# Attention with a depthwise convolution: key blocks in batches of twelve instead of nine

## The chip, the cores and the metric

The kernel runs on one core of a Trainium2 chip. The metric is the device time of one execution in microseconds (us). TensorE (PE) multiplies matrices; its weight loads (PEld) are shown apart. VectorE (DVE), ScalarE (ACT) and GpSimd (POOL) do the rest of the arithmetic, SyncE (SP) only issues DMAs. ScalarE and GpSimd issue DMAs too. Each engine works through its own instructions in order; one that waits holds up everything behind it on that engine.

## The reference

For 4 images `x` of 384 channels and 48 x 48 = 2304 tokens, with 8 heads of 48 channels:

```python
local = conv_general_dilated(x, conv_w, padding='SAME', feature_group_count=C)   # 7 x 7, depthwise
local = local * inv + shift                                                      # batch norm
x_norm = layernorm(x_flat)
q, k, v = split(x_norm @ qkv_w.T + qkv_b)
q = q + layernorm(local_flat)
attn = softmax(q @ k.T * scale)
out = x_flat + (attn @ v) @ proj_w.T + proj_b
```

Everything is float32.

## The kernel before, in words

**Stages.** An image is taken in two stages. The key stage goes through six groups of 384 tokens: keys, values and raw queries are projected (L715), and for images 2 to 4 the output projection of the image before is done beside it. Then the attention goes through five groups of query tokens, of 384 (the first), 480, 480, 480 and 480 columns. The groups are numbered t = 0 to 19 over the four images; t = 0 to 4 are image 1, t = 5 to 19 images 2 to 4.

**Batches.** In one query group each of the four pairs of heads (p = 0 to 3) meets 18 blocks of 128 keys, 72 blocks in all. They are done in 8 batches of 9 blocks, a batch belonging to one pair. A batch has two phases. In `score_batch`, TensorE makes the scores of a block (`score`, L1142): three passes (high x high, high x low, low x high parts in float32r), each for two heads at a time, one head on the upper 64 rows of the array and one on the lower. The two heads' scores take two of the eight PSUM banks, in turn, so four blocks fit. The exponentials go from there to `weights_of` in SBUF: for the first five blocks (`SPLIT`) at once, one ScalarE instruction for both heads (L1158); of the sixth the first half at once; the rest waits in `exps` until weighing. `weights_of` has 11 half-block slots, used in turn. In `weigh_batch`, TensorE multiplies the weights of each block with the values (`weigh`, L1179): full float32, the two heads on the left and right 64 columns of the array. After each `weigh` one waiting exponential is issued, into slots that have become free. The batch's sums are copied out by ScalarE (`sums_out`, L1027 and L1037), and the second part of a pair is added to the first by DVE in the next batch (`sums_add`, L1046).

**Easing.** In some batches (`eased`; all of them for t from 4 on) the third block's second half is copied by DVE from PSUM to SBUF (L1162), and ScalarE makes its exponential in place later (L1154). Scoring then finds the banks free earlier.

**Points.** The order of all engines but GpSimd is written out by hand. Each batch has four points, q = 0 to 3: in mid-scoring, at the end of scoring, in mid-weighing, at the end. `steps_of(t)` hangs other work on points (s, q): the norm of the next image's x (in the last groups of images 1 to 3), the norm of the next group's convolution (`Norm`: sums, a turn through DRAM and back, centring, squares, root, Newton step), query stacks, the division by the softmax sums. At each point `convolve` also issues some of the 7 x 7 convolution for the next group on DVE (L347, 144 instructions a group). How many is worked out ahead by `plan`: every point has a `room` in us (`spare`, and `spare_at_keys` for the key stage's points), a norm needs its group's convolution finished at a due point, and the plan spreads the instructions in proportion to room at the smallest rate that meets the next ten due points.

**Query stacks.** For each pair, `high_queries` (ScalarE, L998) and `low_queries` (DVE, L1003, and DMAs on SP, L1008 and L1010) make a tile `qs` of high, low and shifted parts. The tag `qs` has four buffers, shared with the residuals (`load_residual`) and fetched outputs (`fetch`) of the key stage.

**Keys.** A pair's keys are three stacks of 6 blocks. Three stack tiles are in SBUF; in the key stage pair 0's stacks are made there, those of pairs 1 to 3 are stored to DRAM (`keys_out`, GpSimd's DMAs at L749 to L778). Afterwards `next_keys` loads one stack after another (L787) into the tile whose blocks have been scored. Loads 3 and 4 of each image are issued by ScalarE, all others by GpSimd. `keep_stack` (L782) stores pair 0's stacks for the later groups.

## Time and profile before

| | |
|---|---|
| runs | 2703.12, 2704.47, 2705.36 us; median 2704.47 |
| profiled execution | 2702.29 us, span in the profile 2700.0 us |
| granted TensorE clock | 1.00 |
| TensorE, DVE, ScalarE, GpSimd busy | 2688.3, 2353.5, 1648.4, 599.4 us |
| image 1, attention | from 146.9 to 683.4 us |
| attention of images 2, 3, 4 | from 825.0, 1484.1 and 2141.5 us |

In the tables of groups a row gives line, engine and operation, output and inputs with their shapes, the count, then busy time in us and the mean of one in ns, then the idle time of the engine just before these instructions and what ended it. In a timeline a row is the start in us, the time from the first start to the last end, and what ran how often; square brackets hold the idle time before it and the releaser. Matmuls overlap, so a single one lasts longer than the distance between two.

### The profile page before, as it was taken

What the parts mean: (1) busy time and instruction counts of PE and PEld (TensorE: products, weight loads), DVE (VectorE), ACT (ScalarE), POOL (GpSimd) and SP (SyncE); (2) the same over time, 40 slices, a digit from 0 to 9 for tenths busy, and PEclk for the clock granted to TensorE, in tenths of its full rate; (3) what the DMA queues carried; (4) which work ended last, traced back from release to release, by engine and by line L of the source; (5) the groups of instructions that cost most, each with busy time, mean ns of one, the idle gap of its engine ahead of it and who ended that gap; (6) DMA issues with size and microseconds to landing.
All of it is one profiled execution on the core that took longest, in us unless ns stands there. A gap on an engine that the chain in (4) does not pass through costs nothing.

```text
span 2700.0 us, 45552 instructions
## 1 busy us (share of the span) xinstructions
PE 2688.3 (100%) x16442; PEld 1543.1 (57%) x16442; DVE 2353.5 (87%) x4105; ACT 1648.4 (61%) x2487; POOL 599.4 (22%) x1073
## 2 busy tenths in 40 slices
PE   9999999999999999999999999999999999999999
PEld 6565555555566655555555655555555665555555
DVE  8999999999999999888999999888899899887212
ACT  4466776777325777777622767777753376766662
POOL 4541111102462111011165111101126401110110
PEclk9999999999999999999999999999999999999999
DMA  8454444645465545355456553545636644445442
GB/s 177 93 159 134 132 114 132 154 116 153 125 155 159 141 116 146 117 153 139 123 146 156 155 150 111 150 123 140 150 102 166 166 131 131 139 124 147 136 129 94
DMA packets 160395, 370.43 MB, mean 137 GB/s; under 512 B 58544, under 2 KB 107504, under 8 KB 160160
## 3 DMA queue, kind: packets, MB, share of 16 engines
q0 software_dynamic: 71072, 277.78, 36.3%
q1 hardware_dynamic: 83456, 79.29, 13.1%
q10 hardware_dynamic: 5632, 10.36, 1.2%
q8 instruction: 132, 2.16, 0.3%
q14 instruction: 103, 0.84, 0.1%
HBM read 258.14 MB, written 64.14 MB: 119 GB/s over the span
## 4 chain that ended last, share of the span: by engine, by line
PE 90%; DVE 6%; DMA 2%; issue 1%; ACT 0%; SPq 0%; POOL 0%; DVEq 0%; ACTq 0%; POOLq 0%
PE banks L1179 41%; PE banks L1142 34%; PE banks L715 14%; DVE acc L347 3%; DMA slab<-in_x_dram 0%; DMA staged<-in_qkv_wT_dram 0%; DMA four<-parts 0%; DMA wide<-pt 0%; DVE pt L826 0%; DVE xr L1116 0%; PE banks L605 0%; DMA parts<-part 0%; DVE sq L583 0%; DVE sq L582 0%; DMA qt<-xn 0%
## 5 line engine op out<-in xcount | busy, mean ns | idle before, releaser
L347 DVE SCALAR_TENSOR_TENSOR acc<-slab,vec,acc 128x470 f32<-128x470 f32 (+10 forms) x2832 | 1658.1, 663 | 0.0
L1179 PE MATMUL banks<-pt,v 128*64 128x480 f32 (+1 forms) x5760 | 1150.7, 553 | 1.2 <-ACT pt L1154 1.2
L1158 ACT ACTIVATE pt<-banks 128x960 f32<-128x960 f32 (+1 forms) x1139 | 999.6, 948 | 113.8 <-PE banks L1142 66.6
L1142 PE MATMUL banks<-qs,ks 64*128 64x480 f32 (+1 forms) x8640 | 954.1, 372 | 2.9 <-DVE k L826 1.3
L1142 PEld LDWEIGHTS banks<-qs,ks 64*128 64x128 f32 x8640 | 788.7, 184 | 222.2 <-issue 112.4
L1179 PEld LDWEIGHTS banks<-pt,v 128*64 128x64 f32 x5760 | 399.8, 137 | 674.6 <-issue 625.2
L787 POOL DMA_DIRECT2D ks<-wide x220 | 159.7, 726 | 1471.8 <-PE banks L1142 1463.2
L1154 ACT ACTIVATE pt<-banks 128x480 f32<-128x480 f32 (+1 forms) x461 | 264.8, 574 | 123.3 <-PE banks L1179 117.7
L715 PE MATMUL banks<-xn,w_qk 128*128 128x384 f32 x864 | 284.1, 486 | 0.0
L715 PEld LDWEIGHTS banks<-xn,w_qk 128*128 128x128 f32 x864 | 163.9, 190 | 114.4 <-issue 0.7
L1162 DVE COPY pt<-banks 128x480 f32<-128x480 f32 (+1 forms) x141 | 90.2, 640 | 151.7 <-PE banks L1142 146.6
L1027 ACT COPY o<-banks 113x480 f32<-113x480 f32 (+1 forms) x80 | 43.5, 544 | 206.2 <-PE banks L1179 206.2
L715 PE MATMUL banks<-w_v,xn 128*128 128x384 f32 x432 | 145.1, 488 | 0.2
L809 ACT COPY v<-banks 128x384 f32<-128x384 f32 x72 | 34.2, 477 | 160.5 <-PE banks L715 160.5
L1037 ACT COPY ao<-banks 113x480 f32<-113x480 f32 (+1 forms) x60 | 32.6, 544 | 149.4 <-PE banks L1179 149.4
L715 PEld LDWEIGHTS banks<-w_v,xn 128*128 128x128 f32 x432 | 81.3, 190 | 58.9 <-DVE xn L710 1.9
L1046 DVE TENSOR_TENSOR ao<-ao,o 113x480 f32<-113x480 f32 (+1 forms) x60 | 38.4, 640 | 60.5 <-ACT o L1027 60.0
L1154 ACT ACTIVATE pt<-pt 128x480 f32<-128x480 f32 (+1 forms) x141 | 89.7, 636 | 0.0
L715 PE MATMUL banks<-af,w_o 128*128 128x384 f32 (+1 forms) x270 | 85.2, 470 | 0.0
L772 POOL DMA_DIRECT2D wide<-pt x120 | 60.1, 504 | 112.3 <-ACT pt L823 101.2
L823 ACT ACTIVATE pt<-banks,qkb 128x384 fp32r<-128x384 f32 x60 | 34.7, 581 | 59.2 <-PE banks L715 52.9
L715 PEld LDWEIGHTS banks<-af,w_o 128*128 128x128 f32 x270 | 51.3, 190 | 31.9
(155 smaller groups left out, 1453.8 us busy)
## 6 DMA issues: line engine op xcount, KB each, us to landing
ks<-wide POOLq DMA_DIRECT2D x220, 768.0 KB, 5.1
qs<-qs SPq DMA_DIRECT2D x346, 60.0 KB
slab<-in_x_dram POOLq DMA_DIRECT2D x22, 432.0 KB, 6.4
wide<-ks POOLq DMA_DIRECT2D x12, 768.0 KB, 5.1
xr<-in_x_dram POOLq DMA_DIRECT2D x16, 576.0 KB, 5.5
rb<-rden SPq DMA_DIRECT2D x32, 270.0 KB
held<-ao POOLq DMA_DIRECT2D x12, 720.0 KB, 4.5
xn<-in_x_dram POOLq DMA_DIRECT2D x36, 216.0 KB, 5.1
```

Source lines behind the costliest of these rows:

```text
L347: nc.vector.scalar_tensor_tensor(dst, src, weight, dst, ALU.mult, ALU.add)
L715: nc.tensor.matmul(dst, lhsT=weights(c), rhs=src(c), start=c == 0, stop=c == CC - 1)
L772: nc.gpsimd.dma_start(out=last[16 * u : 16 * u + 16, 0], in_=k[r : r + 16, 0])
L787: queue.dma_start(out=place_keys(b, p, i), in_=wide[b, p][:, :, at])
L823: nc.scalar.activation(k[:, 0, :], r[:, :G], AF.Identity, bias=bias)
L1027: nc.scalar.copy(part[0 : 64 + HA], sums[0 : 64 + HA, :n])
L1046: nc.vector.tensor_add(dst, dst, part[0 : 64 + HA])
L1142: nc.tensor.matmul(r[:, j, :n], lhsT=ks[rows, w, at], rhs=qs[rows, m, :], start=n_th == 0, stop=n_th == 2,)
L1154: nc.scalar.activation(weights_of[:, at, :n], src, AF.Exp, scale=SCALE)
L1158: nc.scalar.activation(to, r[:, :, :n], AF.Exp, scale=SCALE)
L1162: nc.vector.tensor_copy(weights_of[:, second, :n], r[:, 1, :n])
L1179: nc.tensor.matmul(sums[halves[j], :n], lhsT=values[t // NA, kb // NB][:, first : first + 64], rhs=weights_of[:, at[j], :n], start=start, ...
```

## The change

From image 2 on a batch has 12 blocks, and a group 6 batches. A batch no longer belongs to one pair: the second of each three has the last 6 blocks of one pair and the first 6 of the next, and its sums lie in two banks. `SPLIT` becomes 8: eight blocks' exponentials are made before weighing, and 17 half-block slots are kept, six of them in a new tile `more`. Two copies are eased in a batch (blocks 2 and 5). Six points stand in a batch instead of four: ahead of blocks 4 and 8 of scoring, at its end, after 4 and 8 blocks of weighing, at its end. `MOVED` gives each old point (s, q) its new one, so that the steps of a group lie on 36 points; the room at them is new. In image 1 batches stay at nine; two of them (t = 0, s = 5 and t = 3, s = 7) are no longer eased. In the key stage 1.2 us of room go from point (5, 2) to (5, 0).

The tag `qs` with its four buffers is gone. Named places take its stead: two tiles, two parts of `more`, and slots 8 to 10 of `weights_of`. From image 2 on the queries have the two tiles in turn. All loads of keys are issued by GpSimd.

```diff
-BATCH = 9
-SPLIT = 5
-EASED = 2
+FIRST_BATCH = 9
+BATCH = 12
+SPLIT = BATCH - 4
...
+    def batch_of(t):
+        return FIRST_BATCH if t < NA else BATCH
+    def split_of(t):
+        return batch_of(t) - 4
...
-    weights_of = big.tile([P, 2 * SPLIT + 1, GM], F32, tag="pt", name="pt")
+    MOST = 2 * (FIRST_BATCH - 4)
+    weights_of = big.tile([P, MOST + 1, GM], F32, tag="pt", name="pt")
+    def change_more(name, dtype=F32):
+        more[0] = big.tile([P, 2 * CC, GM], dtype, tag="more", name=name)
+    def triple(i, name, dtype=F32):
+        if i < 2:
+            return big.tile([P, CC, GM], dtype, tag=f"triple{i}", name=name)
+        return weights_of[:, 8:11, :] if i == 4 else more[0][:, i % 2 * CC : (i % 2 + 1) * CC, :]
+    def kept(t, at, n=1):
+        if MOST <= at < 2 * split_of(t):
+            return more[0][:, at - MOST : at - MOST + n]
+        at = min(at, MOST)
+        return weights_of[:, at : at + n]
...
     def eased(t, s):
         if t < NA - 1:
-            return s in ((5, 6), (3, 5, 6), (6,), range(1, NBATCH))[t]
-        return True
+            return (2,) if s in ((6,), (3, 5, 6), (6,), range(1, 7))[t] else ()
+        return (2,) if t < NA else (2, 5)
+    MOVED = {
+        (0, 0): (0, 0), (0, 1): (0, 2), (0, 2): (0, 3), (0, 3): (0, 4), (1, 2): (1, 1),
+        (1, 3): (1, 2), (2, 1): (1, 4), (2, 2): (1, 5), (2, 3): (2, 1), (3, 0): (2, 2),
+        (3, 1): (2, 3), (3, 2): (2, 4), (4, 0): (2, 5), (4, 1): (3, 2), (4, 2): (3, 3),
+        (4, 3): (3, 4), (5, 0): (3, 4), (5, 1): (3, 5), (5, 2): (4, 0), (5, 3): (4, 2),
+        (6, 0): (4, 3), (6, 1): (4, 4), (6, 2): (4, 5), (6, 3): (5, 0),
+    }
...
     def spare(t, s, q):
-        time = (2.4, 2.6, 2.8, 3.0)[q]
+        if t < NA:
+            time = (2.4, 2.6, 2.8, 3.0)[q]
+            if q == 0:
+                time -= 0.5 * (s % 2 == 0) + 0.5 * len(eased(t, s))
+        else:
+            time = (1.5, 2.1, 2.6, 2.65, 2.4, 1.7 - 0.5 * (s % 3 > 0))[q]
+        time = max(0.3, time - costs(t).get((s, q), 0.0)) - (0.1 if t >= NA else 0.0)
         return time * columns_of(t) / G
...
-    def load_keys(b, n, queue=nc.gpsimd):
+    def load_keys(b, n):
         p, i = n // 3 % NP, n % 3
...
     def high_queries(t, p):
-        qs = work.tile([P, 3, GM], HALF, tag="qs", name=f"qs{t}_{p}", bufs=4)
+        qs = triple(p if t < NA else 1 - p % 2, f"qs{t}_{p}", HALF)[:, :, : columns_of(t)]
...
+            xr = triple((0, 2, 0, 4, 3, 0)[i] if b < B - 1 else 1, f"xr{b}_{i}")
...
+            ao = triple((1, 4, 3, 1, 2)[i], f"af{b}_{i}")[:, :, : size(at)]
...
-    def score_batch(t, s, middle):
-        p, blocks = blocks_of(s)
-        for i, kb in enumerate(blocks):
-            if i == SPLIT - 1:
-                middle()
+    def score_batch(t, s, *middles):
+        for i, (p, kb) in enumerate(blocks_of(t, s)):
+            if i and i % 4 == 0 and i // 4 <= len(middles):
+                middles[i // 4 - 1]()
             score(t, s, p, kb, i)
...
+    def weigh_batch(t, s, sums, *middles):
+        blocks = blocks_of(t, s)
+        part = 0
+        for i, (p, kb) in enumerate(blocks):
+            begins_here = i == 0 or kb == 0
+            part += begins_here and i > 0
+            ends_here = i == len(blocks) - 1 or kb == KB - 1
+            weigh(sums[:, part, :], begins_here, ends_here)
+            if begins_here:
+                opened = kb
             if exps:
                 exps.popleft()()
+            if ends_here:
+                ended.append((t, p, opened > 0, kb == KB - 1, sums[:, part, :]))
+                sums_out()
+            if i + 1 in turns_of(t):
                 while soon:
                     soon.popleft()()
+                middles[turns_of(t).index(i + 1)]()
+    def turns_of(t):
+        return (5,) if t < NA else (4, 8)
     def next_keys(b, g, s):
-        end = min((g * NP * KB + s * BATCH + BATCH) // THIRD + 3, NP * (KB // THIRD) * NA)
+        n = batch_of(b * NA)
+        end = min((g * NP * KB + s * n + n) // THIRD + 3, NP * (KB // THIRD) * NA)
         while keys_next[b] < end:
-            load_keys(b, keys_next[b], nc.scalar if keys_next[b] < 5 else nc.gpsimd)
+            load_keys(b, keys_next[b])
...
-            sums = score_batch(t, s, lambda: step(0))
+            n = len(turns_of(t))
+            turns = [lambda q=q: step(q) for q in range(2 * n + 1)]
+            sums = score_batch(t, s, *turns[:n])
             next_keys(b, g, s)
-            step(1)
-            weigh_batch(s, t, sums, lambda: step(2))
-            step(3)
+            step(n)
+            weigh_batch(t, s, sums, *turns[n + 1 :])
+            step(2 * n + 1)
```

More of the change, by code (lines that the diff above doesn't have):

```diff
@@ L202, in unshifted_pass @@
     staged = [
-        work.tile([P, CC, GM], F32, tag="qs", name="staged", bufs=4)[:, :, :C] for _ in range(3)
+        triple(i, "staged")[:, :, :C] for i in range(3)
     ]
@@ L273, in unshifted_pass @@
     copies = [
-        work.tile([P, CC, GM], F32, tag="qs", name="copies", bufs=4).rearrange("p c n -> p (c n)")
-        for _ in range(2)
+        triple(i, "copies").rearrange("p c n -> p (c n)")
+        for i in (3, 0)
     ]
@@ L464, in spare, with points_in @@
                 (6, 1): 2.3, (6, 2): 2.5, (6, 3): 0.6,
-            }.get((s, q), 0.0)
-            time -= part * columns_of(t + 1) / columns_of(t)
-        elif t == NA - 1 and (s, q) == (6, 2):
-            time -= 1.3
-        time = max(0.3, time) - (0.1 if t >= NA else 0.0)
+            }
+            todo.append({k: v * columns_of(t + 1) / columns_of(t) for k, v in part.items()})
+        elif t == NA - 1:
+            todo.append({(6, 2): 1.3})
+        total = {}
+        for part in todo:
+            for point, cost in part.items():
+                point = moved(t, *point)
+                total[point] = total.get(point, 0.0) + cost
+        return total
+    def spare(t, s, q):
+        if t < NA:
[5 more added lines that the diff above has]
+        time = max(0.3, time - costs(t).get((s, q), 0.0)) - (0.1 if t >= NA else 0.0)
         return time * columns_of(t) / G
+    def points_in(t):
+        return [(s, q) for s in range(batches_of(t)) for q in range(4 if t < NA else 6)]
     def later(b):
@@ L495, in unshifted_pass @@
             room += [spare_at_keys(t // NA, g, h) for g in range(NG) for h in range(5)]
-        points += [("slot", t, s, q) for s in range(NBATCH) for q in range(4)]
-        room += [spare(t, s, q) for s in range(NBATCH) for q in range(4)]
+        points += [("slot", t, *point) for point in points_in(t)]
+        room += [spare(t, *point) for point in points_in(t)]
     each = CC * KS * KS
@@ L1341, in steps_of @@
             at(7, 1, lambda: low_queries(t + 1, 0, other))
-        return steps
+        in_turn = {}
+        for point in sorted(steps):
+            in_turn.setdefault(moved(t, *point), []).extend(steps[point])
+        return in_turn
     ratios = {}
@@ L1564, in unshifted_pass @@
         steps = steps_of(t)
-        for s in range(NBATCH):
+        for s in range(batches_of(t)):
             def step(q):
```

96 lines of the change are left out of this document (48 added, 48 removed).

## The prediction

> **What bounds the kernel now.** I read the page first (busy shares, then the shares of the chain that ended last), then that chain in time order, then single batches on each engine, last the stages side by side.
>
> ```profile
> span 2700.0 us, 45552 instructions
> PE 2688.3 (100%) x16442; PEld 1543.1 (57%) x16442; DVE 2353.5 (87%) x4105; ACT 1648.4 (61%) x2487; POOL 599.4 (22%) x1073
> PE 90%; DVE 6%; DMA 2%; issue 1%; ACT 0%; SPq 0%; POOL 0%; DVEq 0%; ACTq 0%; POOLq 0%
> ```
>
> TensorE is never out of work: what can be saved is time in which its instructions follow each other more slowly than they need to, and what can be lost is a wait that isn't there today. The chain in images 2 to 4 is a regular alternation of scoring (L1142) and weighing (L1179):
>
> ```profile
> 1062.14 6.05 PE banks L1142 x47
> 1068.19 7.39 PE banks L1179 x36
> 1075.59 4.53 PE banks L1142 x39
> ```
>
> A batch of nine blocks takes 1075.59 - 1062.14 = 13.45 us. Inside one phase (timeline of TensorE, and the mean of one matmul from the groups of that stretch):
>
> ```profile
> 1062.07 0.49 PE L1142 MATMUL banks<-qs,ks 64*128 64x480 f32 x2
> 1062.39 5.58 PE L1142 MATMUL banks<-qs,ks 64*128 64x480 f32 x50
> 1068.57 7.01 PE L1179 MATMUL banks<-pt,v 128*64 128x480 f32 x34
> L1179 PE MATMUL banks<-pt,v 128*64 128x480 f32 x290 | 60.3, 569 | 0.0
> L1142 PE MATMUL banks<-qs,ks 64*128 64x480 f32 x434 | 49.4, 380 | 0.0
> ```
>
> Matmuls run in pairs. 25 scoring pairs take 5.58 with one matmul's 0.38 at the end: (5.58 - 0.38) / 24 = 0.217 us a pair. 17 weighing pairs: (7.01 - 0.57) / 16 = 0.4025. A batch has 27 and 18 of them, 5.85 + 7.25 = 13.10. The other 0.35 us of the 13.45 is the price of going from scoring to weighing and back: part is seen in the first two rows, where the second pair comes 0.32 after the first and not 0.217. No wait is recorded there.
>
> **Fewer switches.** Images 2 to 4 are groups 5 to 19, with 8 batches each, 120 in all; the change makes 6 of twelve blocks, 90 in all. A batch of twelve is 36 x 0.217 + 24 x 0.4025 + 0.35 = 17.82 us, a group 106.9 instead of 107.6. Groups 5, 10 and 15 have 384 columns; their batches lie 1516.87 - 1505.91 = 10.96 apart, with 0.176 a scoring pair (3.68 less one matmul's 0.34, an estimate from the 0.38 above, over 19). I take 0.35 a switch there too, so 12 blocks take about 14.5. The term is 30 x 0.35 = **-10.5 us**; bounds -9, if the shorter streams switch in half of that in the 6 batches concerned, and -11.
>
> ```profile
> 1505.91 5.07 PE L1142 MATMUL banks<-qs,ks 64*128 64x384 f32 x54
> 1516.87 5.06 PE L1142 MATMUL banks<-qs,ks 64*128 64x384 f32 x54
> 1506.72 3.68 PE L1142 MATMUL banks<-qs,ks 64*128 64x384 f32 x40
> ```
>
> **Stalls that the edits outside the batches touch.** Rows with a wait, of ScalarE and of TensorE; the last is a row of the chain:
>
> ```profile
> 167.55 0.53 ACTq L787 DMA_DIRECT2D ks<-wide  x1
> 168.12 0.49 ACT L1154 ACTIVATE pt<-banks 128x384 f32<-128x384 f32 x1 [5.13 <-DMA qt<-xn]
> 163.39 4.08 PE L1179 MATMUL banks<-pt,v 128*64 128x384 f32 x22
> 168.67 2.98 PE L1179 MATMUL banks<-pt,v 128*64 128x384 f32 x14 [1.20 <-ACT pt L1154]
> 209.33 1.85 PE L1142 MATMUL banks<-qs,ks 64*128 64x384 f32 x17 [0.37 <-DVE pt L1162]
> 566.22 2.22 PE L1142 MATMUL banks<-qs,ks 64*128 64x480 f32 x17 [0.89 <-DVE pt L1162]
> 824.95 2.82 PE L1142 MATMUL banks<-qs,ks 64*128 64x384 f32 x19 [1.31 <-DVE k L826]
> 270.05 6.38 PE banks L1142 x54
> ```
>
> In the first image ScalarE stands for 5 us behind a key load that it issues itself (L787), and the exponentials behind it come late: the second part of the weighing of that batch starts 1.2 late by TensorE's row, and the 36 matmuls run from 163.39 to 171.65 (168.67 + 2.98), 8.2 where 10.96 - 5.07 = 5.9 would do; a matmul's tail lies in that, so I count 2.2. With GpSimd issuing, that goes: -2.2. At 209 and 566 a DVE copy (the easing, L1162) is late; both batches are no longer eased. The first gives -0.4; the second loses 0.89 at the wait and a tail of 0.5 with it, 1.4 in all, but an uneased batch costs 0.3 (6.38 at 270, not eased, against 6.05 at 1062), so -1.1. At 825 DVE brings the last low key parts late; the plan moves 1.2 us of room from point 2 to point 0 of the last key group, some three convolution steps that no longer stand ahead of them: -1.3. Together **-5.0**, bounds -6 and -2 (the last two rest on order alone).
>
> **Exponentials.** Longer scoring asks more of ScalarE before weighing: eight blocks instead of five, with two eased instead of one. One batch today:
>
> ```profile
> 1063.09 1.83 ACT L1158 ACTIVATE pt<-banks 128x960 f32<-128x960 f32 x2 [0.35 <-PE banks L1142]
> 1064.81 0.58 ACT L1154 ACTIVATE pt<-banks 128x480 f32<-128x480 f32 x1
> 1065.26 1.86 ACT L1158 ACTIVATE pt<-banks 128x960 f32<-128x960 f32 x2
> 1066.96 0.62 ACT L1154 ACTIVATE pt<-banks 128x480 f32<-128x480 f32 x1
> 1506.83 1.51 ACT L1158 ACTIVATE pt<-banks 128x768 f32<-128x768 f32 x2 [0.32 <-PE banks L1142]
> 1508.23 0.50 ACT L1154 ACTIVATE pt<-banks 128x384 f32<-128x384 f32 x1
> 1508.60 1.54 ACT L1158 ACTIVATE pt<-banks 128x768 f32<-128x768 f32 x2
> ```
>
> The first starts 1.02 after the batch; a full one follows after 0.86, a half (eased) after 0.45. Four pairs of banks mean that block 11 waits for block 7. Block 7 starts at 1.02 + 5 x 0.855 + 2 x 0.45 = 6.20 and takes 1.01: 7.21. TensorE reaches block 11 at 0.10 + 11 x 0.65 = 7.25. Nearly even: +1 for 72 batches (0.015 each). With 384 columns: 0.92 + 5 x 0.695 + 2 x 0.37 + 0.85 = 5.99 against 0.10 + 11 x 0.527 = 5.90; with a few hundredths of hand-over 0.12, in 18 batches +2.2. So **+3.2**; below: 0, if other waits in the same batch hide it; above: +8, if any ScalarE work falls into scoring (0.05 more in each of 90). Squares and query copies are laid on points 2 to 5, behind the scoring.
>
> **DVE.** A group has 12 copies instead of 8, 60 more in all. DVE has room on average:
>
> ```profile
> 914.20:1021.70 107.50, 107.50 (x722) 60.07 (x720) 101.75 (x169) 75.79 (x107) 11.64 (x17) 1.00 0.48 135
> 1344.60:1484.10 139.50, 139.50 (x436) 81.98 (x434) 134.67 (x237) 38.19 (x75) 76.37 (x149) 1.00 0.58 145
> L1162 DVE COPY pt<-banks 128x480 f32<-128x480 f32 (+1 forms) x141 | 90.2, 640 | 151.7 <-PE banks L1142 146.6
> 1096.77 0.17 DVE L702 TENSOR_TENSOR few_u<-few_u,few 128x12 f32<-128x12 f32 x1
> 1099.07 3.62 DVE L347 SCALAR_TENSOR_TENSOR acc<-slab,vec,acc 128x384 f32<-128x384 f32 x6
> 1078.38 0.25 DVE L677 TENSOR_REDUCE few<-four 128x15 f32<-128x60 f32 x1
> 1080.95 2.48 DVE L347 SCALAR_TENSOR_TENSOR acc<-slab,vec,acc 128x450 f32<-128x450 f32 x4
> ```
>
> Columns of the windows are TensorE, weight loads, DVE, ScalarE, GpSimd. Group 6 is 101.75 of 107.5; it gets 4 copies more (0.64 each), but by the plan's arithmetic 124 convolution steps instead of 129 (0.60 each: 3.62 less one of 0.6 over 5), so 101.3 of 106.9. The key stage at 1344 gets 3 more steps, 136.5 of 139.5: hidden, and up to 3 us in all if not. Before 141 copies DVE idles 147 us for TensorE, about 1 us each, so it is early. What counts is the place. After the copy of block 2 (the next work stands at 1078.38, 2.86 after the start at 1062.07 + 13.45) the whole of point 0 stands ahead of the copy of block 5, which has to end by 5.9 for block 9 to start at 5.95. Three or four steps fit (2.86 + 3 x 0.6 + 0.64 = 5.3). In six groups the x norm's end (1096.77 to 1099.07, 2.30) now lies there, with one step in three of them: 2.86 + 2.30 + 0.6 + 0.64 = 6.4, late by 0.5; without it by 0. +1, bounds 0 and 2. In the third batch of groups 5, 10, 15 the query norm's sum (four instructions the size of a copy: 2.6) and centring (1078.38 to 1080.95, 2.57) meet 12 or 13 steps and an addition: 2.6 + 2.6 + 7.5 + 0.6 = 13.3 where the time from one batch's second copy to the next's first is about 12.3: +1 each if nothing else slips; I take **+3** for DVE with the norm's end, bounds 0 and 7.
>
> **Starts of images 2 to 4.** Pair 1's queries and keys are wanted in mid-batch 1, after 14.5 + 0.1 + 6 x 0.53 = 17.8 us, not after two batches (21.9), and both are made later.
>
> ```profile
> 836.80 0.52 POOL L778 DMA_DIRECT2D wide<-k  x1 [1.76 <-DMA qs<-qs]
> ks<-wide POOLq DMA_DIRECT2D x220, 768.0 KB, 5.1
> 1490.06 0.56 DVE L1003 TENSOR_TENSOR qs<-xn,qs 128x384 fp32r<-128x384 f32 x1
> 1494.22 1.93 SPq L1010 DMA_DIRECT2D qs<-qs  x2
> ```
>
> The load of stack 3 goes behind GpSimd's key stores, which in image 2 end at 836.8; some 0.8 earlier it lands at 836 + 5.1 = 841.1, wanted at 824.95 - 1.3 + 17.8 = 841.4. I price it for image 2 alone, where these stores run furthest past the start. Queries: DVE's subtraction (1490.06, 6 us into the image) moves a point on, behind four or five convolution steps more and the second copy, to about 9.6; SP's copies took to 1496.15, 6.1 later; 15.7 and a landing (not in the trace; between 1 and 5, the loads' row) of 2 is 17.7. **+1.5** for both, bounds 0 and 5. The two query stacks add a wait of ScalarE for the residual's store ahead of query 1 and of GpSimd for the old queries; both are released before they are wanted, and cost nothing while the stores land within some 5 us.
>
> The Trainium skill (DMA: Bandwidth & Descriptors, Specifications) speaks against moving the loads: it gives a first byte after about 1 us from GpSimd and 0.6 us from the sync and scalar queues. By it the three loads near the path come 0.4 later each, an estimate from that page of 1.2 us and 2697.9; the trace shows no landing of the ScalarE loads, so no row here tests it.
>
> **Sum.** -10.5 - 5.0 + 3.2 + 3 + 1.5 = -7.8. The profiled execution was 2702.3 with a span of 2700.0; it becomes 2694.5, the span 2692.2. The runs' median (2704.5) is 2.2 above it: **2696.7 us**.
>
> **Rivals.** (1) All pacing holds and every stall above goes: -15.5, 2689.0. For it: waits in one batch hide each other; against: the 384-column count, which comes out late by itself. (2) Break-even, 2702: the terms at their upper bounds (part of them: 8 + 2 + 3 leave -2.5), or the 0.35 is paid per block and not per switch, which leaves -5.0 + 7.7. Against the latter: it is seen between the first two pairs of a phase. (3) Slower: DVE comes late to the *second* copy as a rule, because it is an in-order queue with point 0 between two deadlines 3 us apart. The price is in the row of 566.22: one late copy stretched scoring by 1.4. A convolution step (0.60) too many in half of the 90 batches costs 27: 2704.5 - 15.5 + 27 = 2716.0. It decides from 7.8 / 90 = 0.09 us a batch beyond what I count. For it: one copy was late at 209 and 566; against: the 147 us that DVE waits ahead of its copies.
>
> **Chances.** Forecast 0.47, (1) 0.18, (2) 0.21, (3) 0.14. Anything within 0.2% (5.4 us) counts as no change, which a measurement here can hardly tell apart. Faster is the forecast and (1), 0.65; same 0.21; slower 0.14. The range 2687 to 2705 takes in (1) and (2); the forecast's own is 2691 to 2699.
>
> **What the next profile would show.** Batches in images 2 to 4 17.8 apart (14.5 with 384 columns), scoring x72, weighing x48; no L787 on ScalarE and a second batch of 11.3 in image 1; waits of TensorE for L1158's successor only in groups 5, 10, 15, below 0.2. The forecast is wrong if batches of 480 columns lie above 18.0 apart as a rule, or if the key stages grow beyond 140.

## The result, and the profile after

The kernel as changed takes 2728.2 us against 2703.8 us on the same chip: ratio 1.0092, 95% interval 1.0079 to 1.0104, **24 us slower**. The prediction was 2696.7. The profiled execution took 2728.3 us.

From the page of the changed kernel (its span is 2726.5 us), the engines' busy time:

```profile
PE 2702.6 (99%) x16442; PEld 1549.1 (57%) x16442; DVE 2382.4 (87%) x4163; ACT 1642.6 (60%) x2515; POOL 605.9 (22%) x1081
```

Whom TensorE waited for (total in us, times, longest):

```profile
PE banks L1196 <- DVE pt L1216: 8.1, 4, 4.6
PE banks L1196 <- ACT pt L1212: 5.0, 3, 2.0
...
PE banks L1196 <- DVE more_kept L1216: 1.2, 4, 0.5
PE banks L1196 <- DMA qs<-qs: 0.5, 2, 0.3
```

TensorE waits for scoring's banks (L1196), where it waited for 2.8 us in all before. But these waits are only 14.8 us, and TensorE's busy time grew as well, by 14.3 us, for the same 16442 matmuls. So half of the loss lies in matmuls that follow each other more slowly, with no idle time to be seen. The attention of images 2, 3 and 4 in windows (columns as in the prediction's), of the changed kernel and then of the kernel before:

```profile
824.13:1355.51 531.38, 524.16 (x3602) 300.59 (x3601) 480.01 (x841) 365.00 (x548) 79.10 (x127) 0.99 0.50 135
...
1495.30:2022.15 526.85, 523.11 (x3601) 298.21 (x3600) 476.91 (x836) 364.89 (x548) 77.70 (x125) 1.00 0.50 136
...
2161.67:2686.24 524.57, 521.81 (x3602) 299.71 (x3601) 349.27 (x584) 356.83 (x530) 60.44 (x88) 1.00 0.44 131
```

```profile
824.95:1344.57 519.62, 519.34 (x3600) 298.30 (x3600) 475.19 (x831) 367.10 (x538) 78.97 (x128) 1.00 0.51 139
1484.09:2002.00 517.91, 517.91 (x3602) 297.63 (x3601) 468.02 (x817) 367.04 (x538) 74.67 (x120) 1.00 0.51 138
2141.51:2659.50 517.99, 517.99 (x3602) 297.87 (x3601) 339.22 (x565) 358.31 (x520) 59.37 (x86) 1.00 0.45 133
```

The loss is in the attention of images 2 to 4: 1582.8 us instead of 1555.5, **+27.3**. Of that, 13.4 us is visible idle time (the difference of the two first columns, summed, after minus before), the other 13.9 us are not. Image 1 and the first key stage end 0.8 earlier (824.13 against 824.95); the key stages between the windows are the same to 0.3. Below, a batch's length goes from its first scoring matmul to that of the next.

A batch where nothing goes wrong, in the last group (timeline of TensorE; the last row is block 11, in a stretch of its own):

```profile
2614.41 8.21 PE L1196 MATMUL banks<-qs,ks 64*128 64x480 f32 x72
2622.55 4.25 PE L1234 MATMUL banks<-pt,v 128*64 128x480 f32 x20
...
2632.36 0.92 PE L1196 MATMUL banks<-qs,ks 64*128 64x480 f32 x6
...
2621.70 0.92 PE L1196 MATMUL banks<-qs,ks 64*128 64x480 f32 x6
```

ScalarE's exponentials of blocks 6 and 7:

```profile
2619.75 1.89 ACT L1212 ACTIVATE more_kept<-banks 128x960 f32<-128x960 f32 x2
```

The batch takes 2632.36 - 2614.41 = 17.95 us, not 17.82. Weighing, 2632.36 - 2622.55 = 9.81, is as computed (24 x 0.4025, and the 0.15 of a switch that a weighing phase has in the kernel before too); scoring is 0.14 too long. The row of block 11 is the place: the exponential of block 7 ends at 2619.75 + 1.89 = 2621.64, block 11 starts 0.06 later, and its three pairs take 0.92 where three pairs are 2 x 0.217 + 0.38 = 0.81. By these numbers TensorE reached that block some 0.03 too early, and pays 0.11 on top.

Then the batches that stand out. TensorE:

```profile
1194.80 1.57 PE L1196 MATMUL banks<-qs,ks 64*128 64x480 f32 x6 [4.60 <-DVE pt L1216]
1862.44 1.90 PE L1196 MATMUL banks<-qs,ks 64*128 64x480 f32 x10 [1.96 <-DVE pt L1216]
...
902.80 5.07 PE L1196 MATMUL banks<-qs,ks 64*128 64x384 f32 x48 [1.51 <-ACT pt L1212]
1572.82 4.41 PE L1196 MATMUL banks<-qs,ks 64*128 64x384 f32 x42 [1.52 <-ACT pt L1212]
2240.35 2.12 PE L1196 MATMUL banks<-qs,ks 64*128 64x384 f32 x15 [1.98 <-ACT pt L1212]
```

DVE ahead of the first of them, and ScalarE ahead of the third:

```profile
1190.44 0.25 DVE L726 TENSOR_REDUCE few<-four 128x15 f32<-128x60 f32 x1 [5.84 <-DMA four<-parts]
```

```profile
901.45 0.59 ACT L1048 CAST qs<-xn 128x480 fp32r<-128x480 f32 x1 [1.93 <-DVE xn L1033]
```

In groups 8 and 13 (first two rows) DVE stands 5.84 us (3.72 in group 13) for the query norm's sums, which go through DRAM and back, and the two copies of the next batch are behind it: those batches take 25.6 and 21.8 us. In groups 5, 10 and 15 ScalarE stands at the next group's first query stack (L1048) for an x that DVE is still making, and the exponentials of the batch are behind it: 16.8, 16.8 and 18.6 instead of 14.65.

Three of these batches lose more than they wait. From about the end of the waits of 4.60, 1.96 and 1.98 us on, the granted clock of TensorE, 1.00 elsewhere in the attention of images 2 to 4, stands at 0.50 for 6.8, 3.4 and 3.4 us (windows; the third column from the end is the clock):

```profile
1194.00:1200.80 6.80, 6.00 (x30) 4.98 (x32) 6.80 (x15) 4.16 (x7) 0.00 (x0) 0.50 0.07 23
...
1863.00:1866.40 3.40, 3.40 (x20) 2.90 (x18) 3.40 (x7) 2.59 (x4) 0.00 (x0) 0.50 0.53 198
2241.90:2245.30 3.40, 3.40 (x23) 3.40 (x24) 3.40 (x7) 3.25 (x7) 0.72 (x1) 0.50 0.38 89
```

In the first of them 30 matmuls take 6.00 us, 0.40 a pair instead of 0.217. Over the 12.8 us of work in the three stretches that is a loss of some 6 us (an estimate by these two numbers) that no idle time shows.

The 38.8 us that images 2 to 4 lie above 72 x 17.82 + 18 x 14.5 = 1544.0 are, batch by batch: pacing 72 x 0.14 + 18 x 0.15 = **12.8**; the two batches behind the norm's turn 7.7 + 3.8 = **11.5**; the three behind the query stack 2.1 + 2.1 + 4.0 = **8.2**; eight batches with a late DVE copy or query transfer, 0.4 to 1.1 each, **5.2**; scatter 1.1. The some 6 us at the lower clock are part of the 11.5 and the 8.2. The kernel before is 11.5 above the same 1544.0, so 38.8 - 11.5 = 27.3 is the loss.

### The profile page after: what moved, and what is told of

Read it like the earlier page. It is cut to its first block, busy times and chain, and to the rows that moved or that the text cites. A ratio compares the mean times of both kernels' runs of the same rounds, so it can differ in the third digit from the quotient of the medians.

```text
span 2726.5 us, 45605 instructions
## 1 busy us (share of the span) xinstructions
PE 2702.6 (99%) x16442; PEld 1549.1 (57%) x16442; DVE 2382.4 (87%) x4163; ACT 1642.6 (60%) x2515; POOL 605.9 (22%) x1081
## 3 DMA queue, kind: packets, MB, share of 16 engines
q1 hardware_dynamic: 83456, 79.29, 12.8%
## 5 line engine op out<-in xcount | busy, mean ns | idle before, releaser
L1234 PE MATMUL banks<-pt,v 128*64 128x480 f32 (+1 forms) x4680 | 949.7, 553 | 0.0
L1212 ACT ACTIVATE pt<-banks 128x960 f32<-128x960 f32 (+1 forms) x931 | 815.7, 947 | 88.8 <-PE banks L1196 55.5
L1196 PE MATMUL banks<-qs,ks 64*128 64x480 f32 (+1 forms) x7560 | 849.6, 376 | 13.9 <-DVE pt L1216 6.8
L1196 PEld LDWEIGHTS banks<-qs,ks 64*128 64x128 f32 x7560 | 693.7, 185 | 206.6 <-issue 77.8
L1234 PEld LDWEIGHTS banks<-pt,v 128*64 128x64 f32 x4680 | 325.1, 137 | 546.2 <-issue 531.2
L1234 PE MATMUL banks<-more_kept,v 128*64 128x480 f32 (+1 forms) x1080 | 224.1, 550 | 0.0
L1212 ACT ACTIVATE more_kept<-banks 128x960 f32<-128x960 f32 (+1 forms) x180 | 164.4, 996 | 7.7 <-PE banks L1196 7.6
L1234 PEld LDWEIGHTS banks<-more_kept,v 128*64 128x64 f32 x1080 | 77.7, 137 | 131.0 <-issue 131.0
L1196 PE MATMUL banks<-more_queries,ks 64*128 64x480 f32 (+1 forms) x1080 | 121.5, 374 | 1.3 <-DVE pt L1216 1.3
L1196 PEld LDWEIGHTS banks<-more_queries,ks 64*128 64x128 f32 x1080 | 98.1, 184 | 31.6 <-issue 13.9
```

The lines of the kernel that those rows point to most:

```text
L1196: nc.tensor.matmul(r[:, j, :n], lhsT=ks[rows, w, at], rhs=qs[rows, m, :], start=n_th == 0, stop=n_th == 2,)
L1212: nc.scalar.activation(to, r[:, :, :n], AF.Exp, scale=SCALE)
L1234: nc.tensor.matmul(sums[halves[j], :n], lhsT=values[t // NA, kb // NB][:, first : first + 64], rhs=kept(t, at[j])[:, 0, :n], start=start, ...
```

## The experiments

In the expectations "the kernel of the centring moved" is e2's. Times are medians, and a ratio is to the kernel before, run alongside; a version without a ratio ran once.

### Is it ScalarE's pace? (e1_easing)

```diff
+        if t == NT - 1:
+            return ((1, 3, 5), (1, 3, 5), (2, 5), (2, 5), (2,), (2,))[s]
         return (2,) if t < NA else (2, 5)
```

> The changed kernel, but in the last group (its DVE has no convolution left to do) the batches differ in the blocks that are eased: batches 0 and 1 ease blocks 1, 3 and 5, batches 2 and 3 ease blocks 2 and 5 as before, batches 4 and 5 block 2 alone. Theory (ScalarE's pace: block 11 waits a few hundredths for the exponential of block 7, and the first pair of matmuls after any wait takes 0.11 us longer): batches 0 and 1 take 17.82 us, 2 and 3 17.95, 4 and 5 about 18.37 (0.4 more of exponentials ahead of block 7, all of it waited for). Rival (the switch between scoring and weighing, or scoring itself, costs more in a batch of twelve blocks): 17.95 in batches 0 to 3 alike.

Three batches of the last group, with three, two and one eased block (length, TensorE's busy time, then clock and DMA):

```profile
2576.91:2594.70 17.79, 17.79 (x124) 1.00 0.46 127
2612.51:2630.46 17.95, 17.95 (x122) 1.00 0.31 99
2648.44:2666.79 18.35, 18.35 (x122) 1.00 0.40 140
```

The whole run took 2727.4 us. The batches took 17.8, 17.95 and 18.35: the pace of ScalarE sets the length, and a batch of twelve can take the time that the prediction gave it. In none of the three is any idle time recorded, and the clock is 1.00 in all; a busy column that equals the window doesn't show that TensorE runs at its pace.

### The norm's turn (e2_centre_later, e5_slab_later)

```diff
-        (3, 1): (2, 3), (3, 2): (2, 4), (4, 0): (2, 5), (4, 1): (3, 2), (4, 2): (3, 3),
+        (3, 1): (2, 3), (3, 2): (2, 4), (4, 0): (3, 1), (4, 1): (3, 2), (4, 2): (3, 3),
```

> The changed kernel with one entry of the layout moved: the query norm's centring, from point (2, 5) to (3, 1), half a batch later. Theory (DVE stands for the norm's turn through DRAM and its copies of the next batch come late): the batches at 1185.8 and 1856.1 fall from 25.6 and 21.8 to about 18.0, 11.5 us in all, so 2716.7. Rival (the copies are late because DVE has too much work before them, and the wait only fills a gap): the same work stands half a batch later and those batches, or the ones behind, stay 4 to 7 long; within 2 us of 2728.

2712.3 us, ratio 1.0039 (1.0025 to 1.0053). Both batches fell to 17.98, 11.5 us as expected. Another 5 us came from groups 5 and 15: the fourth batch, whose copies had stood behind the centring too, fell from 15.7 to 14.7 in each, and the sixth from 16.8 to 15.2 and from 18.6 to 17.3. In group 5 the sixth batch's wait is gone. In group 15 the wait is as long as before (TensorE's row in e2 below), and what is gone is the lower clock: it is 1.00 in e2's whole batch.

```profile
2225.51 5.07 PE L1196 MATMUL banks<-qs,ks 64*128 64x384 f32 x48 [1.99 <-ACT pt L1212]
```

One line of a table of points cost the change 16 us, in waits and in the clock behind them.

Why the turn was late (SP's own rows; the changed kernel, with the turn behind it, then the kernel before with a turn of its own):

```profile
1176.09 0.59 SPq L716 DMA_DIRECT2D parts<-part  x1
1187.80 0.60 SPq L717 DMA_DIRECT2D four<-parts  x1
1188.50 0.55 SPq L716 DMA_DIRECT2D parts<-part  x1
1190.78 0.55 SPq L717 DMA_DIRECT2D four<-parts  x1
```

```profile
1287.16 0.59 SPq L667 DMA_DIRECT2D parts<-part  x1
1297.75 0.59 SPq L668 DMA_DIRECT2D four<-parts  x1
```

SP sends the sums, and the fetch behind them starts when they have landed, 11.7 us later; DVE has them 14.4 us after the store was sent (12.3 in group 13). The kernel before has such turns too (10.6 here), but nobody waits: its layout leaves more than a batch between sum and centring, where the changed one leaves half a batch. So the turn didn't become slow; the layout stopped covering it. Whether the store is slow because GpSimd has large loads under way then (two of keys and parts of a slab, the image rows that the convolution reads, from 1172.4 to 1187.5) e5 was to tell.

```diff
-SLAB_AT = 40
+SLAB_AT = 56
```

> The changed kernel with the slab's loads sixteen convolution steps later, so that GpSimd doesn't send them just behind two key loads. It asks whether the query norm's turn through DRAM comes late because its small store lands behind those loads (collision), or because half a batch is too short for the turn in any case. Collision: the stores of the two groups land 2 to 5 us after their issue instead of 11, the batches at 1185.8 and 1856.1 take 18.0, and the time is 11 us less, 2717. Turn too short: the stalls of 7.7 and 3.8 us stay, or show in other groups, and the time stays within 2 us of 2728.

2727.6 us, and it tells nothing: the loads weren't moved. GpSimd sends a slab when its buffer comes free, not when the step is laid, so they stand where they stood (GpSimd in e5, released by DVE), and SP's turn takes 11.2 us again:

```profile
1170.77 0.59 POOL L149 DMA_DIRECT2D slab<-in_x_dram  x1 [2.92 <-DVE acc L374]
```

```profile
1175.29 0.60 SPq L716 DMA_DIRECT2D parts<-part  x1
1186.48 0.60 SPq L717 DMA_DIRECT2D four<-parts  x1
```

The collision is a likely cause and stays an argument. For it speaks that the next turn, sent at 1188.5 when those loads had landed, took 2.3 us. The Trainium skill (DMA: Bandwidth & Descriptors, Queues, rings and completion order) says that a DMA engine takes turns between the queues at packet granularity, which would let a small store wait behind other queues' packets; no run here separates it.

### The query stack of groups 5, 10 and 15 (e3_queries_later, e8_taps_later, e12_taps_earlier)

```diff
+        if t >= NA and t % NA == 0 and point in ((6, 2), (6, 3)):
+            return (5, 1) if point == (6, 2) else (5, 2)
         return point if t < NA else MOVED[point]
```

> The changed kernel with the next group's first query stack made later in the groups with 384 columns only (5, 10, 15): high part from point (4, 5) to (5, 1), low part from (5, 0) to (5, 2). Theory (ScalarE stands at that high part for the x that DVE still makes, and the exponentials of the next batch behind it come late): the batches at 898.9, 1568.9 and 2236.0 fall from 16.8, 16.8 and 18.6 to about 14.7, 8.2 us in all; up to 0.6 comes back at the start of the next group; 2720.0 to 2720.6. Rival (DVE is too full there, so what is late is its own copies): the wait only moves to a copy by DVE, and at most 2 us are saved.

2737.9 us, ratio 1.0138 (1.0122 to 1.0155): 10 us worse than the changed kernel, where both theories said better or the same. The next group starts without its queries (SP's last copies for them, then TensorE):

```profile
910.14 1.22 SPq L1062 DMA_DIRECT2D qs<-qs  x2
```

```profile
920.57 4.77 PE L1198 MATMUL banks<-qs,ks 64*128 64x480 f32 x22 [3.75 <-DMA qs<-qs]
```

SP's copies are sent until 911.4 and TensorE gets them at 920.6: the transfers behind the stack need some 9 us, and I had allowed for the arithmetic alone. (Behind this wait, too, the granted clock stands at 0.50 for 6.8 us.) The step can't go later; it has to be made sooner, so its input must come sooner.

```diff
-            if i == len(order) - AHEAD and t + 1 < NT:
+            if i == len(order) - (AHEAD if t < NA or t % NA else 16) and t + 1 < NT:
```

> The kernel of the centring moved to (3, 1), with the first taps of ScalarE asked for 16 instead of 24 steps before the end in the groups with 384 columns, so that the root of the query norm is no longer behind them. Theory (ScalarE is late with the root, DVE's chain of 4.6 starts late, and the query stack's high part holds ScalarE at the start of the next batch): the root runs 2.1 earlier, the batches at 1558.4 and 2221.2 take 14.7 to 14.9 instead of 16.8 and 17.3, 4.5 us in all, 2708. Rival (DVE has convolution steps ahead of that chain and starts it when it did before): they stay at 16.5 or more.

The first taps are the start of a group's convolution, which ScalarE makes. 2716.1 us, and no answer: this `t` is the group being convolved, two ahead of the one in attention, so other groups' taps were moved. The batches in question still had them ahead of the norm's root and took 16.8 and 18.6. e12 moves the right ones, and sooner:

```diff
-            if i == len(order) - AHEAD and t + 1 < NT:
+            if i == len(order) - ({12: 34, 17: 48}.get(t, AHEAD)) and t + 1 < NT:
```

> The kernel of the centring moved to (3, 1), with the first taps that stood ahead of the query norm's root in groups 10 and 15 asked for earlier (34 and 48 steps before the end of the convolution concerned instead of 24), so that they run half a batch before the root. Theory (ScalarE is late with the root by those 2.15 us, DVE's chain starts late, the query stack holds ScalarE): the batches at 1558 and 2221 fall from 16.8 and 17.3 to 15.2 at most, as in group 5, where the taps stood earlier anyway: 3 to 4 us in all. Rival (DVE's convolution steps hold the chain): 16.5 or more.

2707.0 us, 5 below e2. The two batches fell from 16.8 and 17.3 to 15.22 and 15.21, which is 3.6 of the 5. So the chain was: first taps (2.15 us) ahead of the root on ScalarE, DVE's chain of 4.6 us late by as much, the query stack late, ScalarE's exponentials late. 0.6 us of each is left.

### The key loads in image 1 (e4_before_gpsimd_keys)

```diff
-            load_keys(b, keys_next[b], nc.scalar if keys_next[b] < 5 else nc.gpsimd)
+            load_keys(b, keys_next[b])
```

> The kernel before with one edit of the change alone: the key loads that ScalarE issued are issued by GpSimd too. The prediction's step: the batch at 157.7 falls from 13.5 to 11.3, and the attention of image 2 starts 2.2 earlier than 824.95, at 822.75. Rival (DVE is the bound of image 1, as it is busy for 109 of the 111 us of the second group, and TensorE only waits for it later): the batch falls just the same, but waits for DVE in the same group or the next take it back, and image 2 starts at 824.5 to 825.

The kernel before with this edit alone (TensorE):

```profile
158.95 5.39 PE L1142 MATMUL banks<-qs,ks 64*128 64x384 f32 x54
...
170.22 5.38 PE L1142 MATMUL banks<-qs,ks 64*128 64x384 f32 x54
...
209.78 1.84 PE L1142 MATMUL banks<-qs,ks 64*128 64x384 f32 x17 [2.17 <-DVE pt L1162]
```

The batch falls from 13.5 to 11.27, as the step said, and four batches later TensorE waits 2.17 for DVE where it waited 0.37: 1.8 of the 2.2 are given back within the group. Image 2 starts at 824.87 instead of 824.95. The rival held, as far as one execution shows it: DVE bounds that stretch, and ScalarE's stall was cover.

### Can the pace be mended? (e7, e9, e10, e11, e13, e14, e16, e17)

All of these stand on e2. e7 lets DVE copy one whole block (both banks, in one instruction) instead of two halves:

```diff
-        return (2,) if t < NA else (2, 5)
+        return (2,) if t < NA else (4,)
...
+        if i in eased(t, s) and t >= NA:
+            both = kept(t, first, 2)[:, :, :n]
+            nc.vector.tensor_copy(both, r[:, :, :n])
+            copied.append(lambda: nc.scalar.activation(both, both, AF.Exp, scale=SCALE))
...
-            if i and i % 4 == 0 and i // 4 <= len(middles):
-                middles[i // 4 - 1]()
+            turns = (4,) if t < NA else (5, 8)
+            if i in turns:
+                middles[turns.index(i)]()
```

> The kernel of the centring moved to (3, 1), and in images 2 to 4 DVE eases one whole block (block 4, both of its banks in one copy) in place of half of block 2 and half of block 5; the step between the blocks stands behind block 4. ScalarE then has 6 x 0.855 instead of 5 x 0.855 and 2 x 0.45 ahead of block 7's exponential: it ends 0.05 sooner, at 7.18, where a start of block 11 at 7.25 is no longer late by the 0.05 of hand-over. Theory (pacing by ScalarE with a restart behind it): batches with 480 columns 17.83 instead of 17.97, 72 x 0.13 = 9.4 less, those with 384 columns 14.60 to 14.65; the second copy's late places (up to 0.8 in five batches) go too, 2 us; 2701 to 2703. Rival (the copy of 960 columns, about 1.2, holds the banks of block 8 or comes late as often as the two did): 17.9 to 18.1 a batch, 2710 to 2716.

2712.7 us, ratio 1.0039 (1.0025 to 1.0052): nothing gained. In the last group a batch takes 17.90; block 11 no longer waits, but block 7 now does, for the exponential of block 3, fourth in ScalarE's row: the four ran from 2600.16 to 2603.72, and block 7 was due at 2603.78, with the hand-over still between; its first pair took 0.30. I had left out that an exponential ends 0.15 after the next may start. The sixth batches of groups 6 to 8 and 11 to 13 came out 0.5 to 1.2 longer than in e2 as well, behind DVE's query chain.

> The three edits together: centring at (3, 1), one whole block eased, first taps later in the groups with 384 columns. If the three causes are separate, 28.2 (the kernel as changed) less 16, 11 and 4.5: 2697, some 6 below the kernel before and near what the prediction's first two terms gave. If they hide each other, 2701 or more.

e9 (e7 and e8 together): 2712.7 us, ratio 1.0040 (1.0026 to 1.0054), since neither of its two new parts did its work.

e10 is e7 with block 3 in place of 4 and the points where they were:

> The kernel of the centring moved to (3, 1), and in images 2 to 4 DVE eases the whole of block 3 (in e7 it was block 4, and block 7 waited there for the exponential of block 3, which ended at 4.585 where 4.65 less the hand-over was wanted). With block 3 out of ScalarE's row the blocks before are 0, 1, 2, then 4 to 7; by e7's own times block 2 ends at 3.72 (wanted by 4.0), block 4 at 4.59 (by 5.30), block 7 at 7.17 (by 7.25), and the copy runs from 3.0 to 4.2 (by 4.65). Theory (pacing by ScalarE and DVE, a restart of 0.1 after each wait): batches with 480 columns of the last group 17.80 to 17.83 as with three eased halves, 72 x 0.14 = 10 less than the kernel with the centring alone, with the copy late in the nine or so batches where it was late in e7 (5 us back): 2706 to 2708. Rival (a long copy by DVE slows TensorE's banks or the exponentials by itself): 17.9 or more in the last group, 2711 or more.

2708.3 us, ratio 1.0022 (1.0013 to 1.0032). 17.90 again in the last group, although no block starts late by more than 0.01: block 11 starts on time, and its first pair still takes 0.08 more. The rival had the 17.9, but not for this reason.

e11 adds e12's taps and takes convolution from ahead of the query norm's root:

```diff
-                (2, 3): 2.6, (4, 0): 1.4, (4, 1): 1.0, (4, 2): 2.0, (4, 3): 0.5, (6, 0): 0.4,
+                (2, 3): 2.6, (4, 0): 1.4, (4, 1): 1.0, (4, 2): 2.0, (4, 3): 0.5, (6, 0): 1.6,
```

> The whole block 3 eased, the taps earlier in groups 10 and 15, and 1.2 us less convolution laid at point (4, 3), ahead of the query norm's root, so that DVE's chain behind the root starts when the root is there (one or two convolution steps between the mean and the root's product instead of four to six). From 2707 for the block alone: less 4 for the taps, less 3 to 5 for the late copies and query stacks of the fifth batches, 2698 to 2700, below the kernel before by 0.1 to 0.2%. Rival (the steps taken out of (4, 3) make DVE late elsewhere): 2705 or more.

2703.9 us, ratio 1.0005 (0.9996 to 1.0014). Images 2 to 4 take 1555.3 us, what they took before the change, but image 2's attention starts 5.5 later than in e10 (829.12 against 823.67): the plan, with less room later, had asked for five more convolution steps in image 1's attention (749 against 744). Some 1.6 us of the 5.5 are the clock, which stands at 0.50 from 223.6 to 227.0 (weighing pairs 0.64 apart instead of 0.32), behind a wait of 1.93 for DVE (1.31 in e10). e13 gives the room back elsewhere:

```diff
-            time = (1.5, 2.1, 2.6, 2.65, 2.4, 1.7 - 0.5 * (s % 3 > 0))[q]
+            time = (1.5, 2.3, 2.6, 2.65, 2.4, 1.7 - 0.5 * (s % 3 > 0))[q]
```

> The kernel of e11 with the 1.2 us of room that were taken from point (4, 3) given back at point 1 of every batch in images 2 to 4 (2.3 instead of 2.1), so that image 1 isn't asked for more convolution: e11 had two to four steps more there and its image 1 took 4.2 us more. Theory: image 2's attention starts at 823.7 instead of 829.1, images 2 to 4 keep 518.1 to 518.7: 2699. Rival (image 1's 4.2 us is not from those steps): 2702 to 2704.

2702.4 us, ratio 0.9996 (0.9987 to 1.0005): image 2 starts at 824.85, with 744 steps in image 1 and the clock at 1.00 there, so those steps it was, directly and by way of the clock. That is 3 us short of the 2699 expected; half of it is the batch at 2247.1 in group 16, 19.5 long for a query transfer that comes 1.24 late.

e14 asks what the last 0.1 of a batch is, by taking 0.08 us from ScalarE ahead of block 7:

```diff
+        elif t >= NA and i == 2:
+            to, rest = kept(t, first, 2), 48 if n == GM else 96
+            thin = to[:, :, n - rest : n]
+            nc.scalar.activation(to[:, :, : n - rest], r[:, :, : n - rest], AF.Exp, scale=SCALE)
+            nc.vector.tensor_copy(thin, r[:, :, n - rest : n])
+            copied.append(lambda: nc.scalar.activation(thin, thin, AF.Exp, scale=SCALE))
```

> The kernel of e13, and in images 2 to 4 DVE also copies the last 48 columns (96 where a block has 384) of both banks of block 2, whose exponentials ScalarE makes later: some 0.08 us (0.16) less of ScalarE ahead of block 7. It asks what is left of the 0.1 between the 17.90 of e10's last group and the 17.80 of three eased halves, where TensorE is not seen to idle, yet the first pair of block 11 takes 0.08 more. Theory (a wait of a hundredth is enough to make the first pair behind it 0.08 to 0.11 longer): 17.80 in the last group, 72 x 0.1 and 18 x 0.15 less, 2690 if DVE has the time, 2693 if some copies come late. Rival (the longer first pair belongs to the batch and not to the wait): 17.90 as before, and the time within 2 us of e13's.

2739.3 us, ratio 1.0130 (1.0114 to 1.0145): 0.42 more in every batch. DVE's small copy waited for ScalarE's exponential of the same block (their targets lie interleaved in the same slots; I take that for the reason, and no run shows it), and the whole copy behind it held block 7. A batch of 18.3 against 17.9 from one copy 0.9 late shows how little room the banks leave, but not what was asked. e16 takes the strip from block 1:

> e14 with the thin copy taken from block 1 in place of block 2. In e14 DVE's thin copy started only at 3.67, when ScalarE's exponential of the same block had ended (3.64), and pushed the copy of block 3 to 4.99, so block 7 came 0.4 late in every batch. From block 1 the exponential ends near 2.78, the thin copy at 3.06, the copy of block 3 at 4.22 (wanted by 4.57). Theory (a wait of a hundredth costs 0.08 to 0.1 by the slower first pair): 17.80 in the last group, 72 x 0.1 and 18 x 0.1 less than e13: 2693 to 2695. Rival (the price belongs to the batch): 17.90, 2702.

2707.9 us, ratio 1.0017 (1.0008 to 1.0027), 5 worse than e13. Its batches are of two kinds. Two of the last group (DVE):

```profile
2596.65 0.26 DVE L1222 COPY pt<-banks 128x96 f32<-128x96 f32 x1 [5.79 <-ACT pt L1221]
2596.82 0.65 DVE L1096 TENSOR_TENSOR ao<-ao,o_True 113x480 f32<-113x480 f32 x1
2597.39 1.15 DVE L1216 COPY pt<-banks 128x960 f32<-128x960 f32 x1
...
2632.69 0.26 DVE L1222 COPY pt<-banks 128x96 f32<-128x96 f32 x1 [9.45 <-ACT pt L1221]
2632.86 1.15 DVE L1216 COPY pt<-banks 128x960 f32<-128x960 f32 x1
```

Where the sums of a pair are added between the two copies (second row), the copy of block 3 ends 4.71 us into the batch, later than block 7 is due (4.65), and the batch takes 18.03; where they aren't, it ends at 4.12, and the batch takes 17.83, where e13's take 17.89 to 17.91. So the 0.1 does go with a little less of ScalarE: it is no price of the longer batch.

e17 is e13 with half of block 2 eased as well, right ahead of the whole block 3:

```diff
-        return (2,) if t < NA else (3,)
+        return (2,) if t < NA else (2, 3)
```

> e13 with half of block 2 eased as well, right ahead of the whole of block 3, in all of images 2 to 4: 0.4 less of ScalarE ahead of block 7, 0.64 more of DVE in each batch (3.8 in a group, where e13's DVE idles 7 to 11 of 107). Theory: 17.80 and 14.50 a batch, 9 us less than e13, of which DVE gives back up to 5 where its chains stand: 2693 to 2699. Rival (DVE's room is all in places where it isn't wanted): late copies as in the changed kernel, 2702 or more.

**2698.6 us, ratio 0.9984 (0.9975 to 0.9993)**: 4.5 us faster than the kernel before, and the only version whose interval lies below 1; by the prediction's own measure (0.2%) it is still no change. Attention of images 2 to 4 in windows; the last block of a batch of the last group (TensorE); the exponential of its block 7 (ScalarE):

```profile
824.69:1340.92 516.23, 516.17 (x3601) 297.32 (x3601) 492.57 (x836) 365.17 (x518) 77.62 (x125) 1.00 0.51 138
1480.44:1997.61 517.17, 516.32 (x3601) 296.71 (x3601) 489.58 (x832) 365.26 (x518) 78.74 (x127) 1.00 0.51 138
2137.13:2654.50 517.37, 516.45 (x3602) 297.78 (x3601) 363.06 (x582) 357.21 (x500) 60.18 (x87) 1.00 0.45 133
```

```profile
2590.39 0.84 PE L1196 MATMUL banks<-qs,ks 64*128 64x480 f32 x6
```

```profile
2589.26 0.99 ACT L1212 ACTIVATE more_kept<-banks 128x960 f32<-128x960 f32 x1
```

The exponential of block 7 ends 0.14 before block 11 starts (2590.25, 2590.39), and the three pairs take 0.84 instead of 0.92. 65 of the 72 batches with 480 columns lie between 17.81 and 17.85, the plain ones with 384 columns at 14.53. The three images take 1550.8, 4.8 less than before, though DVE is busier by 17 to 24 us in each. What is above 72 x 17.84 + 18 x 14.53 = 1546.0 is in eleven longer batches, 4.8 in all.

## Why the prediction was wrong, step by step

The span came out 26.5 us longer (2726.5 against 2700.0) instead of 7.8 shorter. Two steps failed: the exponentials' wait was charged too little (12.8 us instead of 3.2), and the term for DVE put at nothing the time that a norm's turn and a query stack need between two steps (19.7 us, some 6 of them by the lower clock).

**Fewer switches, -10.5: right in size, and not what decides.** The 17.82 and 14.5 are met (17.84 and 14.53 in e17, 17.79 with three eased blocks in e1), weighing took 9.81 as counted. A switch does cost the 0.35.

**Exponentials, +3.2 with an upper bound of 8: the step that failed by size.** It measured 12.8: 2.7 in the 18 batches with 384 columns, where 2.2 was forecast, and 10.1 in the 72 with 480, where it was 1. The arithmetic of starts and ends was right to 0.05 (block 7's exponential due to end at 7.21 and TensorE at block 11 at 7.25; measured 7.23, and 7.26 where nothing is late, in e17; block 11 then started at 7.29, some 0.05 behind the exponential). What failed is the price: the step charged the length of the wait, 0.015, and this wait costs its length and some 0.1 more. Two rows that the prediction had quoted point that way: 0.32 instead of 0.217 at the start of a phase, which it took for the switch's own, and 6.38 against 6.05 in an uneased batch. The bound of 8 was built on "some ScalarE work falls into scoring", not on the wait that the sum already had.

**Stalls outside the batches, -5.0: -0.8 measured**, by the start of image 2's attention (e1, e2, e3, e8 and e12, whose edits lie behind image 1, start it between 823.56 and 824.97, so it is 0 to -1.4). e4 shows why for its largest term: the 2.2 were paid out and taken back by DVE within five batches. The step had put a stall's end down as a gain without asking what was late next, in the one stretch where DVE was busy for nearly the whole time. Of the other three terms no run separates the parts. In the changed kernel the waits of 0.37, 0.89 and 1.31 are gone, but at 215 and 221 us TensorE waits 1.25 and 1.31 for DVE where it didn't before.

**DVE, +3 (0 to 7): 5.2 of its kind, and 19.7 of another.** The late copies that it named are there (the fourth batch of groups 5, 10 and 15 +1.0, +0.4 and +1.1, behind the centring at the end of the third; the norm's end +0.5 in group 7 and 0.1 to 0.4 in five more). What it didn't have are the two waits at the head of DVE's and ScalarE's queues: it counted the instructions of the moved norm steps, but not that the time *between* two steps, in which a transfer runs, became shorter. Point (4, 0) went to (2, 5), half a batch behind the sums; from the store to DVE's next step it took 14.4 and 12.3 us there. The trace before shows such turns (10.6 from store to fetch, covered), and the prediction looked at SP's row only for the query copies. The query stack in groups 5, 10 and 15 (8.2) is the same error one engine on: a cast on ScalarE with exponentials queued behind it. And no term of the sum had a price for the clock: behind three of these waits it stood at 0.50.

**Starts of images 2 to 4, +1.5: 0.5.** TensorE waited for queries 0.34 in image 2's second batch, which was 0.5 longer; its other wait for them (0.16) lies in group 16. The 2 us that the step took for the landing of the last query copies were a choice; in e3 TensorE started 9.2 us after these copies were sent.

**The rivals.** The slower one (2716.0, chance 0.14) had the sign, and its mechanism in part: DVE's copy is late and what stands ahead of it in an in-order queue is the cause. But it is not the rule: eight of 90 batches wait for a copy, 8.2 us in all, and the two that matter stand behind a transfer, not behind convolution steps. The rule was the other thing, in all 90 batches, and invisible as idle time. The break-even rival named the bound of 8 + 2 + 3 and stopped where its bounds stopped. (The range, 2687 to 2705, was narrower than the terms: their upper bounds together, -9 - 2 + 8 + 7 + 5, give +9 and 2713.5. And the 0.35 paid per block, -5.0 + 7.7, gives 2707, not 2702.) The sentence on the Trainium skill (DMA: Bandwidth & Descriptors, Specifications; 0.4 later per load from GpSimd) would have given 2697.9; e4, which moves just those loads, starts image 2 no later (824.87 against 824.95) and ends no later (2700.7 against 2702.6), so nothing of it is seen here, and the landing of a load that ScalarE issues is in no trace.

**What would have shown it** was named rightly: the forecast was to be wrong if batches of 480 columns lay above 18.0 as a rule. They lay at 17.96, where the whole saving of 0.7 us a group was already gone (6 x 17.96 = 107.8 against 107.6); the threshold should have been worked out from the saving, which a mere 0.12 a batch eats up.

## What to carry to other kernels

When a change lengthens a pipeline's batch to save a fixed price, work out the slack of every hand-over in the new batch, and charge a near miss with its restart, not with its length; a time that comes out "nearly even" is a loss. When steps are moved, check the time between a store and the step that needs it back as well as the steps' own cost, and ask of each instruction that may wait what stands behind it on its engine. Read the granted clock beside the waits, stretch by stretch: a mean of 1.00 hides a stretch at half. A stall that goes on one engine is worth what the next-slowest engine leaves of it in that stretch, which one run of that edit alone shows.

## What was not expected of the hardware

TensorE pays for a wait that the profile doesn't record as idle: the first pair of scoring matmuls behind it took 0.08 to 0.11 us longer (three pairs 0.92 in the changed kernel, 0.84 in e17), even where the block started within 0.01 us of its due time (e10, where the exponential it needs ended 0.08 before; in e17 it ended 0.14 before). That is 0.5% of a batch, in every batch. The Trainium skill (TensorE: Matmul & The Clock Gate, Step-by-step: what each phase is for) has the matching rule, that matmuls follow each other at the pace of their columns only because the next one already stands at the array's input while the last drains; for a wait in such a stream that section gives no price, only one for a matmul that stands alone, and the 0.1 here is this case's.

The granted clock fell to 0.50 behind some waits of about 2 us and not behind others. In the changed kernel it stood there for 3.4 us behind waits of 1.96 and 1.98, and the batch of the second was 4.0 us longer than the plain 14.65; in e2 the same batch waited 1.99, the clock stayed at 1.00, and it was 2.6 longer. In e1 it stayed at 1.00 behind a wait of 2.29. Behind the waits of 4.60 here and 3.75 in e3 it stood at 0.50 for 6.8 us. What decides in the shorter ones no run here shows.

ScalarE's exponentials of 960 columns follow each other after 0.85 to 0.87 but end 0.97 to 1.04 after their start, so the last result of a row of them is 0.10 to 0.19 later than the distances add up to; e7 was laid out wrongly by just that.
